# Bias reads at the end of step 4 over two queues, later residual requests, and earlier weight sums in two pairs

## The chip, the cores and the metric

The kernel runs on one core of a Trainium2 chip. The core has TensorE (PE, matrix products; PEld is its weight load), VectorE (DVE), ScalarE (ACT), GpSimd (POOL) and SyncE (SP), each with its own instruction queue that is worked off in order. SP only issues transfers here; ACT issues some too. The metric is the device time of one execution in microseconds; less is better. The profile comes from one further execution, with its own time beside the span that it records.

## The reference

Two layers, each: group normalization of the input (32 groups of channels over the image), attention with relative positions over 32 x 32 = 1024 tokens, output projection, and the input added back. There are 4 images, 768 channels, 12 heads of 64.

```python
def _L0_conv_ref(x, Wqkv, Wproj, bproj, rel_pos_h, rel_pos_w):
    ...
    qkv = x @ Wqkv
    ...
    rel_h = jnp.einsum('bhwc,hkc->bhwk', r_q, Rh)
    rel_w = jnp.einsum('bhwc,wkc->bhwk', r_q, Rw)
    bias = rel_h[..., :, None] + rel_w[..., None, :]
    ...
    scores = scale * jnp.einsum('bqc,bkc->bqk', q, k) + bias
    attn = jax.nn.softmax(scores, axis=-1)
    out = jnp.einsum('bqk,bkc->bqc', attn, v)
    ...
    return out @ Wproj + bproj
...
x = x + _L0_conv_ref(_gn(x), L0_conv_Wqkv, L0_conv_Wproj, L0_conv_bproj, L0_conv_rel_pos_h, L0_conv_rel_pos_w)
x = x + _L1_conv_ref(_gn(x), L1_conv_qkv_w, L1_conv_qkv_b, L1_conv_proj_w, L1_conv_proj_b, L1_conv_rel_pos_h, L1_conv_rel_pos_w)
```

Layer 1 differs by a bias on q, k and v and by a second factor of the scale. Everything is float32.

## The kernel before

**Pairs and steps.** The work is 8 images in a row (4 of layer 0, then 4 of layer 1), 6 pairs of heads in each: 48 pairs, numbered g = 0 to 47; `pair` is g % 6. A pair has 8 steps n = 0 to 7, one for each 128 query tokens. The main loop (from L719) goes over the 384 units (g, n). It is software pipelined by hand: the order in which the program issues work is the order on every engine, except where dependencies between engines make them wait.

**A step.** In step n of pair g the loop issues, in this order:
- what the lists `early` and `later` hold: a closure put into `later` runs at the start of the step after next, one put into `early` at the start of the next;
- until the change, the requests for weights and residuals of the output projection (`fetch_weights`, L578, and `fetch`, L595);
- `biases` (L454) of the unit two ahead: POOL adds the two relative position terms into a 128 x 1024 score tile;
- `scores` (L468) of the unit one ahead: PE multiplies q and k into PSUM (`ps_s`, two tiles, one for each head), DVE adds the bias and finds the minimum (L484), ACT takes the exponential (L488);
- `read_back` calls kept in `behind` and `behind2`;
- `turn` (L506): DVE transposes the finished weights of unit n into `tb`; in odd steps SP writes `tb` to DRAM (`td`, L521). Between the two heads DVE inverts the next unit's sums (L495);
- `divide` (L497) of the unit one ahead, one head on POOL (L502), one on ACT (L504);
- projections of the next pair and output groups of the image before or of this image, taken from the list `todo` by `take`, as many matmul slices as `shares[n]` says;
- one or two entries of `last`, the copies of the first bias term into place by `rows_axis` on ACT (L431).

**Quarters.** Two steps make a quarter. The quarter is written to DRAM in an odd step and read back turned round (`td` to `pt`, L531) in the second step after for quarters 0 and 2, in the next one for quarters 1 and 3. `weigh` (L536) multiplies quarters 0 and 1 with v at the end of step 6, quarters 2 and 3 at the end of step 2 of the next pair. So quarter 1 is written in step 3, read back in step 4 and used in step 6.

**Relative positions.** `positions` (L396) of the next pair runs in steps 2 and 3: PE multiplies q with the tables, ACT copies the result out (L418) and writes the part for one axis to DRAM (`tdr`, L420). `diagonals` (L437) then reads that back along diagonals into `rel_of[g][2]`, eight transfers of 32 KB in runs of 128 bytes (L447). Their first reader is `biases` of the next pair's unit 0, on POOL in step 6.

**Output groups.** An image's output projection is cut into groups of 128 channels by 512 tokens; four of them are taken in step 7 of every pair from g = 3 on. Each needs a 256 KB residual (`res`), added on DVE (L638, L640). Tiles of `res` share a pool of four with the copied positions.

**Weights.** For pairs that are not `plain` the projections use combined weights: `sum_weights` (L321) gives an ACT copy (L330) and three POOL sums (L333 to L335). A DVE copy (L274) and the projections of the next pair read them. The first three pairs of image 0 have no output groups.

## Time and profile before

| what | value |
|---|---|
| median of 3 runs | 3508.94 us (3507.96 to 3512.74) |
| the profiled execution | 3509.05 us, span 3507.3 us |
| busy in the span | PE 97%, DVE 75%, POOL 71%, ACT 57% |
| DMA traffic | 1051.56 MB, 300 GB/s on average |
| transfers td, written | 384 on SP, 1024 KB each, 5.9 us from issue to landing |
| transfers pt, read back | 382 on SP, 1024 KB each, 7.7 us |
| transfers rel, bias reads | 380 on SP and 4 on ACT, 32 KB each, 3.1 and 2.2 us |
| transfers tdr | 94 on ACT, 256 KB each, 4.8 us |

In the views, a line of a group gives the kernel's line, engine, operation, what it writes and reads, and how often; then busy time, mean duration, the idle time of the engine just before, and what ended it. In a timeline the first column is the start from the beginning of the span in us, the second the duration of the merged group, and a bracket at the end holds the idle time before it and what ended that. SPq and ACTq are the sequencers that issue transfers; the duration of an issue is not that of the transfer.

### The profile page before, as it was taken

How to read it: one execution, taken by the hardware profiler on the slowest of the kernel's cores; microseconds unless marked ns; L12 is line 12 of the kernel's file. 1: busy time of each engine (PE TensorE's matmuls, PEld its weight loads, DVE VectorE, ACT ScalarE, POOL GpSimd, SP SyncE). 2: the span in 40 equal slices, each digit the busy share in tenths (PEclk: the TensorE clock that was granted, in tenths of full speed). 3: DMA queues.
4: the chain of work that ended last, by engine and by line, in shares of the span. 5: the costliest groups of instructions: out<-in, count | busy, mean ns of one | idle time of the engine just before them, and what ended most of it. 6: DMA issues, size and time to landing. Idle time of an engine off the chain costs nothing.

```text
span 3507.3 us, 56203 instructions
## 1 busy us (share of the span) xinstructions
PE 3404.6 (97%) x20652; PEld 1906.9 (54%) x20652; DVE 2640.3 (75%) x4011; ACT 1992.0 (57%) x3958; POOL 2489.6 (71%) x1510
## 2 busy tenths in 40 slices
PE   6899999999999999999999999999999999999999
PEld 4455555555555555555555555555555555555554
DVE  4687868778688786787777877777876778777776
ACT  3565556555565556556665566555665566555652
POOL 3876687766866769767686766876678766786663
PEclk9999999999999999999999999999999999999999
DMA  3678988898889887888888898888988889888888
GB/s 115 252 274 321 330 288 307 310 323 327 290 302 328 318 317 270 318 320 320 296 288 316 303 324 289 299 312 302 319 305 300 297 304 327 298 303 299 305 292 289
DMA packets 531221, 1051.56 MB, mean 300 GB/s; under 512 B 143872, under 2 KB 206848, under 8 KB 481792
## 3 DMA queue, kind: packets, MB, share of 16 engines
q1 hardware_dynamic: 476448, 1020.53, 81.0%
q10 hardware_dynamic: 54496, 27.43, 2.6%
q8 instruction: 163, 2.67, 0.3%
q14 instruction: 114, 0.93, 0.1%
HBM read 572.73 MB, written 475.10 MB: 299 GB/s over the span
## 4 chain that ended last, share of the span: by engine, by line
PE 66%; ACT 12%; DMA 8%; DVE 6%; POOL 3%; issue 3%; SPq 1%; ACTq 0%; DVEq 0%; POOLq 0%
PE pj L268 17%; PE av L550 14%; PE s L475 13%; PE o L629 13%; PE pv L376 7%; ACT sc L488 6%; DMA pt<-td 5%; ACT rel L431 3%; ACT sc L504 2%; PE tp L408 2%; DMA td<-tb 2%; DVE x L228 1%; DVE sc L484 1%; DVE tb L518 1%; POOL x L346 1%
## 5 line engine op out<-in xcount | busy, mean ns | idle before, releaser
L461 POOL TENSOR_TENSOR sc<-rel,rel 128x1024 f32<-128x1024 f32 x768 | 1553.3, 2086 | 110.3 <-DVE tb L518 67.6
L488 ACT ACTIVATE sc<-sc,sm 128x1024 f32<-128x1024 f32 x768 | 879.7, 1147 | 927.2 <-DVE sm L484 925.5
L518 DVE STREAM_TRANSPOSE tb<-sc 128x1024 f32<-128x1024 f32 x768 | 944.8, 1234 | 145.4 <-DMA td<-tb 143.8
L484 DVE CUSTOM_DVE_ANT_0 sc<-s,sc 128x1024 f32<-128x1024 f32 x768 | 908.3, 1221 | 149.8 <-PE s L475 141.4
L502 POOL TENSOR_SCALAR sc<-sc,sm 128x1024 f32<-128x1024 f32 x384 | 429.5, 1119 | 804.1 <-DVE sm L495 792.0
L268 PE MATMUL pj<-x,w 64*128 64x512 f32 x4140 | 937.3, 596 | 57.1 <-DVE x L228 26.1
L475 PE MATMUL s<-k,q 64*128 64x512 f32 x3072 | 749.0, 597 | 6.1 <-DVE sm L484 5.9
L550 PE MATMUL av<-pt,v 128*64 128x256 f32 x6144 | 707.5, 383 | 22.8 <-DMA pt<-td 22.8
L268 PEld LDWEIGHTS pj<-x,w 64*128 64x128 f32 x4140 | 421.7, 189 | 545.0 <-issue 451.5
L550 PEld LDWEIGHTS av<-pt,v 128*64 128x64 f32 x6144 | 445.4, 138 | 314.1 <-DMA pt<-td 46.5
L504 ACT ACTIVATE sc<-sc,sm 128x1024 f32<-128x1024 f32 x384 | 441.0, 1148 | 173.6 <-DVE sm L495 173.6
L376 PE MATMUL pv<-wv,x 64*128 64x256 f32 x4608 | 515.1, 376 | 6.8 <-DVE k L243 6.8
L376 PEld LDWEIGHTS pv<-wv,x 64*128 64x128 f32 x4608 | 449.5, 187 | 98.1 <-issue 38.0
L629 PE MATMUL o<-attn,wo 128*128 128x512 f32 x1080 | 478.9, 598 | 4.3 <-DMA wo<-in_wo 1.3
L475 PEld LDWEIGHTS s<-k,q 64*128 64x128 f32 x3072 | 291.5, 187 | 295.9 <-issue 261.8
L431 ACT COPY rel<-t 32x64 f32<-32x64 f32 x1504 | 363.4, 242 | 16.5
L629 PEld LDWEIGHTS o<-attn,wo 128*128 128x128 f32 x1080 | 200.3, 190 | 279.7 <-issue 250.4
L418 ACT COPY t<-tp 128x512 f32<-128x512 f32 x188 | 110.1, 585 | 223.1 <-PE tp L408 169.5
L346 POOL TENSOR_TENSOR x<-x,x 64x512 f32<-64x512 f32 x144 | 183.3, 1292 | 39.6 <-ACT x L348 28.7
L495 DVE RECIPROCAL sm<-sm 128x2 f32<-128x2 f32 x384 | 60.1, 156 | 176.4 <-ACT sc L488 172.4
L243 DVE TENSOR_TENSOR k<-pj,k 128x512 f32<-128x512 f32 x173 | 116.3, 681 | 68.8 <-PE pj L268 44.0
L488 ACT ACTIVATION_READ_ACCUMULATOR sc<-sc,sm 128x1 f32 x768 | 143.2, 186 | 0.0
(54 smaller groups left out, 1575.8 us busy)
## 6 DMA issues: line engine op xcount, KB each, us to landing
td<-tb SPq DMA_DIRECT2D x384, 1024.0 KB, 5.9
pt<-td SPq DMA_DIRECT2D x382, 1024.0 KB, 7.7
w<-in_wqk SPq DMA_DIRECT2D x96, 384.0 KB, 4.8
tdr<-t ACTq DMA_DIRECT2D x94, 256.0 KB, 4.8
x<-in_x SPq DMA_DIRECT2D x84, 256.0 KB, 7.4
part<-res SPq DMA_DIRECT2D x84, 256.0 KB, 5.6
res<-part SPq DMA_DIRECT2D x84, 256.0 KB, 7.8
wv<-in_wv SPq DMA_DIRECT2D x24, 768.0 KB, 13.5
```

Of the source, the lines that this page charges most:

```text
L268: nc.tensor.matmul(t[:, a, :], lhsT=w[a][rows, c, :], rhs=x[c][rows, :], start=(c == 0), stop=(c == len(x) - 1),)
L376: nc.tensor.matmul(t[:, a, k, :], lhsT=xs[i // 2 * NC + c][rows, at * P : (at + 1) * P], rhs=w[rows, c, :], start=(c == 0), stop=(c == NC ...
L431: nc.scalar.copy(rel[of, :, j, :], t[of, j, :, at : at + HW])
L461: nc.gpsimd.tensor_tensor(sc.rearrange("p (a k) (u l) -> p a l (k u)", a=4, l=8), rel0[:, h, :].unsqueeze(1).unsqueeze(2).to_broadcast(shape),
L475: nc.tensor.matmul(ps[h][:, cols], lhsT=q[rows, n * P : (n + 1) * P], rhs=k[rows, cols], start=True, stop=True,)
L484: nc.vector.tensor_tensor_reduce(out=sc, in0=ps[h], in1=sc, scale=-scale, scalar=BIG, op0=ALU.add, op1=ALU.min, accum_out=st[:, 0, h : h + 1],
L488: nc.scalar.activation(sc, sc, AF.Exp, bias=st[:, 0, h : h + 1], scale=-1.0, accum_out=st[:, 1, h : h + 1],)
L502: nc.gpsimd.tensor_scalar(sc, sc, st[:, 2, h : h + 1], 1.0, ALU.mult, ALU.mult)
L504: nc.scalar.activation(sc, sc, AF.Copy, scale=st[:, 2, h : h + 1])
L518: nc.vector.transpose(tb[:, :, j, :], sc_of[g, n, h])
L550: nc.tensor.matmul(av[rows, at * 2 * P : (at + 1) * 2 * P], lhsT=v_of[g][:, k, rows], rhs=pt_of[g, quarter, h][:, :, k, :], start=(k == 0) ...
L629: nc.tensor.matmul(t, lhsT=wo_of[im, o, c], rhs=attn_of[im * NP + c, i], start=(c == c0), stop=(c == c1 - 1),)
```

## The change

Three edits. First, `diagonals` of the next pair is put into a list of its own, `diagonal`, which is run at the end of step 4 and no longer at its start; the four reads of the second head are issued by ACT for every pair, not for pair 0 alone. Second, the requests for output weights and residuals stand behind the bias adds, the scores and the read back in their step, and the second pair of residuals is requested in step 6 and no longer in step 5. Third, the weights of the pair two ahead are combined in steps 5 and 6, no longer in 6 and 7, where g is below 3 and the next pair is not plain, which is for pairs 1 and 2.

```diff
--- before.py
+++ after.py
@@ -432,7 +432,7 @@
 
         last.extend([lambda: rows_axis((0, 1)), lambda: rows_axis((2, 3))])
         if i == 1:
-            later.append(lambda: diagonals(g))
+            diagonal.append(lambda: diagonals(g))
 
     def diagonals(g):
         td = t_of[g]
@@ -444,7 +444,7 @@
                     td.tensor, td.offset + HW * y * P + h * D + HW - 1,
                     [[P - 1, HW], [P * P, NT], [1, HW]],
                 )
-                (nc.scalar if h and not g else nc.sync).dma_start(
+                (nc.scalar if h else nc.sync).dma_start(
                     out=rel_of[g][2][32 * y : 32 * y + 32, h, :, :], in_=src
                 )
 
@@ -655,7 +655,7 @@
 
 
 
-    early, mid, later, last, behind, behind2 = [], [], [], [], [], []
+    early, mid, later, last, diagonal, behind, behind2 = [], [], [], [], [], [], []
 
     def run(todo):
         while todo:
@@ -705,7 +705,7 @@
         take(todo, NC)
         mid.pop(0)()
         run(last)
-        later.pop()()
+        run(diagonal)
         take(todo, 2 * NC)
         run(early)
         run(later)
@@ -746,11 +746,6 @@
             run(early)
             early, later = later, early
 
-            upto = 4 * (pair % 3) + 3
-            if n in (2, 4, 5) and (im, pair) >= (0, 3):
-                upto -= 2 if n == 4 else 0
-                (fetch_weights if n == 2 else fetch)(place[((im, 0) if pair >= 3 else (im - 1, 1)) + divmod(upto, 2)])
-
             ask = [divmod(g + 3, NP)] if n == 1 else []
             if im == 0 and pair < 3:
                 ask = [(0, 2 * pair + n // 4)] if n in (1, 4) else []
@@ -766,6 +761,11 @@
                 scores(*units[at + 1])
             run(behind)
             behind, behind2 = behind2, behind
+
+            upto = 4 * (pair % 3) + 3
+            if n in (2, 4, 6) and (im, pair) >= (0, 3):
+                upto -= 2 if n == 4 else 0
+                (fetch_weights if n == 2 else fetch)(place[((im, 0) if pair >= 3 else (im - 1, 1)) + divmod(upto, 2)])
             if pair == 3 and n in stages and not end:
                 stages[n]()
             share = shares[n]
@@ -782,11 +782,15 @@
                         take(todo, 3)
                         share -= 3
                     apply(c % NC, c // NC)
-            if g + 2 < NPAIR and not plain(g + 2) and n in (6, 7):
-                if n == 6:
+            if g + 2 < NPAIR and not plain(g + 2):
+                k = n - (5 if g < 3 and not plain(g + 1) else 6)
+                if k == 0:
                     combine = sum_weights(g + 2)
-                combine[n - 6]()
+                if k in (0, 1):
+                    combine[k]()
             take(todo, share)
+            if n == 4:
+                run(diagonal)
             for k in range(min(len(last), 2 if n == 3 else 1)):
                 last.pop(0)()
             if pair == NP - 2 and n == 7 and not end:
```

## The prediction

> **What bounds the kernel now.** I read the page's busy times first, then the waits, then timelines of steps 4 to 7 of two pairs. From the page, busy times and the row of the weighted sums:

> ```profile
> PE 3404.6 (97%) x20652; PEld 1906.9 (54%) x20652; DVE 2640.3 (75%) x4011; ACT 1992.0 (57%) x3958; POOL 2489.6 (71%) x1510
> ...
> L550 PE MATMUL av<-pt,v 128*64 128x256 f32 x6144 | 707.5, 383 | 22.8 <-DMA pt<-td 22.8
> ```

> TensorE is idle for 102.7 us of 3507.3; only that, and matmuls slowed by idling, can be won. I measured each step on TensorE from one score block's start to the next. In a common pair of either layer the steps take 6.97, 10.33, 9.87, 6.87, 6.90, 6.90, 8.87, 12.41 us, again and again; above all step 6, where quarters 0 and 1 are weighed, varies. Over pairs 1 to 46 its excess above 8.87 sums to 44.7 us: 26.1 in the eight pairs numbered 4, 18.6 in the rest (0.5 each). Step 7 adds 6.1 in four of the pairs 4. Pair 28 shows why; timeline of SP, then of TensorE (start, duration, last the wait):

> ```profile
> 2099.96 1.79 SPq L521 DMA_DIRECT2D td<-tb  x2
> 2101.84 3.42 SPq L117 DMA_DIRECT2D x<-mid  x3
> 2105.35 4.95 SPq L447 DMA_DIRECT2D rel<-tdr  x8
> 2111.10 0.35 SPq L131 DMA_DIRECT2D w<-in_wqk  x1
> 2111.55 0.85 SPq L608 DMA_DIRECT2D res<-mid  x2
> 2112.46 0.97 SPq L531 DMA_DIRECT2D pt<-td  x2
> ```

> ```profile
> 2117.45 4.22 PE L550 MATMUL av<-pt,v 128*64 128x256 f32 x34
> 2123.72 5.35 PE L550 MATMUL av<-pt,v 128*64 128x256 f32 x30 [2.05 <-DMA pt<-td]
> ```

> Quarter 1's transposed weights went out at 2099.96 and 2101.42 and had landed at 2107.45, but SP asked for them back at 2112.46, after eight bias reads and two residuals; the second landed at 2123.68 and TensorE waited. After the wait 30 matmuls took 5.35 us; the granted clock of that step is 0.87.

> [...] bias reads cost 0.45 us each on SP (median) and 0.47 on ACT (the first pair's four). [...] ACT at pair 4's first position block:

> ```profile
> 368.47 0.59 ACT L418 COPY t<-tp 128x512 f32<-128x512 f32 x1 [3.24 <-PE tp L408]
> 371.54 0.37 ACTq L420 DMA_DIRECT2D tdr<-t  x1
> 371.95 0.58 ACT L418 COPY t<-tp 128x512 f32<-128x512 f32 x1 [2.89 <-DMA td<-tb]
> ```

> The copy ended at 369.05, yet the issue came at 371.54, when an unrelated write (td, landed 371.46) was done. By the transfers' records all 1,992 transfers of SP and ACT share eight semaphores in rotation: each issue waits until the transfer eight before it has landed. SP shows it too: three of the bias reads above are issued at the landings of the three x loads eight places earlier.

> **The change, part by part.** Time 0 is the start of step 4's scores in pair 26 (1961.25).

> (a) Bias reads. Before: eight issues, 6.24 us of SP, then the read back at 8.4 and 8.8, landed 17.0 and 19.6; quarter 1 is first used at about 19.2 (13.8 for step 6, 1.9 for scores, 3.5 for quarter 0). After: the writes land at 3.6 and 6.1, and the reads go then. A read with little ahead lands 5.7 to 6.4 us after issue (2089.39 to 2095.77), the second follows 2.7 later: 9.6 and 12.3. That is 7 us early: step 6's wait goes, 44.7 us, with step 7's 6.1.

> The price is on ACT. Four issues of 0.47 are 1.9 us a pair, 47 x 1.9 = 88 in all, behind step 4's division and ahead of eight bias copies and step 5's exponentials. ACT in pair 26:

> ```profile
> 1968.04 1.15 ACT L504 ACTIVATE sc<-sc,sm 128x1024 f32<-128x1024 f32 x1 [0.23 <-DVE sm L495]
> 1969.10 2.01 ACT L431 COPY rel<-t 32x64 f32<-32x64 f32 x8
> 1971.88 1.15 ACT L488 ACTIVATE sc<-sc,sm 128x1024 f32<-128x1024 f32 x1 [0.78 <-DVE sm L484]
> ...
> 1978.34 1.15 ACT L488 ACTIVATE sc<-sc,sm 128x1024 f32<-128x1024 f32 x1 [2.69 <-DVE sm L484]
> ```

> The 0.78 and 2.69 us of idle hide 1.9. They don't hide the semaphores. Ahead of the eight bias reads now stand, in order of issue: tdr, td, td, w, pt, pt, res, res. So the first four reads find their semaphores free, and the last four wait for pt, pt, res, res: 9.6, 12.3 and, residuals landing 0.65 apart, 12.9, 13.6. SP is ready for its four at about 7 (just after the second read and two residual issues), ACT at 7.9 to 9.4; so the last place is probably ACT's. Its fourth issue ends near 14.1 instead of the block being over at 9.8. Then copies 2.0 (16.1), two exponentials 2.4 (18.5; before 13.0). Behind them: VectorE's reciprocal and second transpose 1.35, four value adds 1.65 (21.5), the two score evacuations 2.4 (h = 0 done 22.7, h = 1 23.9; before 15.8 to 18.2). TensorE wants the second score bank at 22.9: 1.0 us late. The lateness still stands on VectorE in step 7, where the third or fourth output group waits 0.3 to 0.9 for its bank. I take 1.4 a pair. A precedent bounds it below: in pairs numbered 3 the exponentials of step 5 already end at 15.7 (a square root in step 4), and TensorE's step 6 is at its 8.87 there in pairs 21 and 39. So the first 3 to 4 us of delay are free.

> In pairs numbered 4 VectorE also normalizes inputs in steps 6 and 7 and is the tighter engine: evacuation in step 7 ended 6.5 us before the next scores in pair 28 (33.1, 39.6). With the hold near 15 it ends at about 34.2, so 40.7 against a best of 35.1: 5.6 lost. Pairs numbered 5 have a step 4 of 13.2 us: no loss.

> POOL needs the reads for step 6's bias adds at 14.4; they land near 16. Its four units of work there fill 7.78 of 9.48 us and the sums are used only at 25: nothing, unless the reads are over 6 us late.

> (b) Operands. Two residual requests move from step 5 to step 6, and all behind the read back. Eight issues in a pair stay eight. Before, SP stood up to 3.5 us at L608 for bias copies on ACT (40.8 us in all), hidden because the next write waits for VectorE anyway. Residuals requested near 15 to 21 land by 29; the adds that use them come after 30. Cost 0; if that cover went, 0.7 a group.

> (c) Weights. Pairs 1 and 2 alone: one ACT copy (0.83) and three POOL sums (1.80 each) come a step sooner. Their step 7 is 3.4 us, with no output groups. POOL, VectorE and TensorE at pair 2:

> ```profile
> 213.51 1.79 POOL L335 TENSOR_TENSOR w<-w,w 64x768 f32<-64x768 f32 x1
> 215.27 3.95 POOL L461 TENSOR_TENSOR sc<-rel,rel 128x1024 f32<-128x1024 f32 x2
> ```

> ```profile
> 215.34 4.09 DVE L274 COPY w<-w 64x384 f32<-64x384 f32 x1 [3.38 <-POOL w L335]
> ```

> ```profile
> 219.48 9.84 PE L268 MATMUL pj<-x,w 64*128 64x512 f32 x36 [3.51 <-DVE w L274]
> ```

> The sums would end at 207, the copy could start when VectorE is free at 212.4, and would again run beside bias adds[...] (4.09 us, median 0.59). So it ends by 216.5 instead of 219.4: 3 us a pair, 6 in all. Bounds: 0 and 14 (step 1 is 17.56 there, 10.33 elsewhere).

> **Sum, against the profiled run's 3509.05** (span 3507.3 and 1.75 around it; the median of three is 3508.94, the same). Off: 44.7 + 6.1 + 6. On: 31 pairs at 1.4 = 43, seven at 5.6 = 39, the last loaded pair (46) 1.4: 84. Net +27: 3536 us.

> **Rivals.**
> - *ACT goes first.* If ACT's four stand before SP's, or its last no later than the place that waits for the second pt (12.3), the exponentials end by 17.1 and nearly all is covered. SP then waits instead, with nothing urgent behind it. 3509.05 - 56.8 + 3 = 3455. The rotation of semaphores is fixed before the run, and in the old trace it departs from the order of issue times by up to 3 us between the two engines; ACT would need some 1.5. This is the case on the other side of no change.
> - *The two cancel.* A hold that ends near 13, or only in some kinds of pair: half of the 84 and all of the gain would be 3494, three quarters 3515; I put it at 3504.
> - *VectorE can't catch up.* If lateness outlives step 7 into the next pair, or the idle lowers the clock as in pair 28 (0.87), 3 a pair rather than 1.4 gives about 3586.
> - *The read back is no earlier.* Were it limited by its bytes, nothing would be won; but 12.3 against 19.6 leaves 7 us.

> **How the numbers follow.** ACT held 0.57 (own range 3512 to 3568, from 0.6 to 2.4 us a pair), ACT first 0.25, cancelling 0.12, no catching up 0.06. Some 0.2% (7 us) is what a measurement can tell from no change: of the held case 0.06 lies within it, of the cancelling one 0.06 within and 0.03 on each side. Faster 0.28, same 0.12, slower 0.60. For 8 in 10 the range must reach into the fast case: 3452 to 3566.

> **What would show it.** Right: the reads of pt in step 4 issued within 1 us of the writes' landing; step 6's wait on pt near 0; gaps of 3 to 5 us on ACT ahead of L447; waits of scores on VectorE growing from 6 us to over 25. Wrong: no gap on ACT at L447, a hold under 3 us, or waits of POOL on the bias reads.

## The result and the profile after

The changed kernel takes 3654.59 us (median; 3653.83 to 3655.51), the kernel before, run beside it, 3510.84. The ratio is 1.0409, with a 95% interval of 1.0391 to 1.0427: 144 us slower, where 27 were predicted, and outside the range of 3452 to 3566.

From the page of the changed kernel, the busy times and the rows that answer to those of before:

```profile
PE 3472.9 (95%) x20652; PEld 1913.6 (52%) x20652; DVE 2648.2 (73%) x4011; ACT 1997.1 (55%) x3958; POOL 2486.2 (68%) x1510
...
L475 PE MATMUL s<-k,q 64*128 64x512 f32 x3072 | 792.2, 610 | 46.5 <-DVE sm L484 46.1
L550 PE MATMUL av<-pt,v 128*64 128x256 f32 x6144 | 707.8, 388 | 48.1 <-DVE v L391 47.0
...
L431 ACT COPY rel<-t 32x64 f32<-32x64 f32 x1504 | 363.7, 242 | 262.1 <-DMA rel<-tdr 207.6
```

Three things are to be seen. The weighted sums hardly wait for the read-back (1.2 us, once; 22.8 us before): that part worked. They wait 47.0 us for value tiles from VectorE instead, and the scores wait 46.1 us for score banks (5.9 before). And TensorE is *busy* 68.3 us longer with the same 20,652 matmuls: its mean granted clock fell from 0.996 to 0.979. The bias copies on ACT stand behind 262.1 us of idle time, against 16.5 before. The rows of the scores and of the copies before the change:

```profile
L475 PE MATMUL s<-k,q 64*128 64x512 f32 x3072 | 749.0, 597 | 6.1 <-DVE sm L484 5.9
L431 ACT COPY rel<-t 32x64 f32<-32x64 f32 x1504 | 363.4, 242 | 16.5
```

Measured step by step on TensorE, as in the prediction, the two traces differ by 144.5 us: 66.6 in step 6, 67.5 in step 7, 8.4 in step 1, little elsewhere. An odd pair shows the chain. Pair 25, timeline of SP and then of ACT (start, duration, engine, line, last the wait); its step 4 starts at 1965.80:

```profile
1968.70 3.66 SPq L531 DMA_DIRECT2D pt<-td  x2
1972.46 0.95 SPq L608 DMA_DIRECT2D res<-part  x2
1973.46 2.08 SPq L447 DMA_DIRECT2D rel<-tdr  x4
```

```profile
1974.48 0.37 ACT L388 COPY v<-pv 128x256 f32<-128x256 f32 x1 [0.49 <-DVE v L391]
1975.85 6.59 ACTq L447 DMA_DIRECT2D rel<-tdr  x4
1982.49 2.02 ACT L431 COPY rel<-t 32x64 f32<-32x64 f32 x8 [7.63 <-DMA rel<-tdr]
```

SP's four reads go out in 2.08 us. ACT's four, of the same size, take from 1975.85 to 1982.44. By the transfers' records they are issued at 1975.85, 1980.34, 1981.49 and 1982.14; the transfers eight places before them, two read-backs and two residuals, land at 1975.83, 1980.32, 1981.47 and 1982.12. ACT is held until 16.6 us into step 4, with eight copies and two exponentials behind it. TensorE in the same pair, and then in pair 26:

```profile
1981.40 7.13 PE L550 MATMUL av<-pt,v 128*64 128x256 f32 x64
1991.06 4.91 PE L475 MATMUL s<-k,q 64*128 64x512 f32 x8 [2.53 <-DVE sm L484]
1995.90 12.13 PE L629 MATMUL o<-attn,wo 128*128 128x512 f32 x24
```

```profile
2057.71 2.81 PE L550 MATMUL av<-pt,v 128*64 128x256 f32 x24
2063.09 6.22 PE L550 MATMUL av<-pt,v 128*64 128x256 f32 x40 [2.57 <-DVE v L391]
```

In the odd pair TensorE idles 2.53 us for the score bank; then eight score matmuls take 4.91 us (1.99 in pair 26) and 24 output matmuls 12.13 (10.57). Those two excesses, 2.92 and 1.56, are all of the 4.49 us by which step 7 is over its 12.41; 1.14 of it is the second score bank, which VectorE frees at 1992.14, one evacuation after the first (an evacuation is VectorE's reading of a finished bank, which frees it: the first ends at 1990.99, and the scores start at 1991.06). In the even pair TensorE stops in the middle of the weighted sums, for a value tile. The granted clock in four of these stretches (window; length; busy time of each engine; then the clock, the DMA share and GB/s):

```profile
2063.09:2069.24 6.15, 6.15 (x40) 3.59 (x41) 5.45 (x9) 4.00 (x6) 4.79 (x4) 0.72 1.02 343
1979.59:1988.53 8.94, 8.94 (x74) 5.09 (x70) 1.31 (x2) 5.71 (x14) 1.32 (x2) 1.00 0.47 149
1991.06:1995.90 4.84, 4.82 (x9) 1.46 (x9) 4.69 (x8) 4.34 (x6) 3.39 (x3) 0.62 0.99 324
1995.90:2007.96 12.06, 12.06 (x26) 5.12 (x25) 8.41 (x14) 3.53 (x5) 7.66 (x6) 0.87 0.66 260
```

In pair 25 the clock is 1.00 ahead of the idle time and 0.62 and 0.87 behind it; in pair 26 it is 0.72 behind it. In pair 28, shown of before, all 64 weighted sums are now one run; and for part (c), pair 2's projection waits 1.43 us for the combined weight instead of 3.51 (TensorE again, two stretches):

```profile
229.39 2.85 PE L268 MATMUL pj<-x,w 64*128 64x512 f32 x12 [1.43 <-DVE w L274]
...
2208.68 7.13 PE L550 MATMUL av<-pt,v 128*64 128x256 f32 x64
```

### The profile page after: what moved, and what is told of

Its sections match the earlier page's. It is cut to its first block, busy times and chain, and to the rows that moved or that the text cites. A ratio compares the mean times of both kernels' runs of the same rounds, so it can differ in the third digit from the quotient of the medians.

```text
span 3652.2 us, 56214 instructions
## 1 busy us (share of the span) xinstructions
PE 3472.9 (95%) x20652; PEld 1913.6 (52%) x20652; DVE 2648.2 (73%) x4011; ACT 1997.1 (55%) x3958; POOL 2486.2 (68%) x1510
## 4 chain that ended last, share of the span: by engine, by line
PE 27%; DMA 8%; ACT 8%; DVE 4%; issue 2%; POOL 2%; SPq 0%; ACTq 0%; DVEq 0%; POOLq 0%
PE o L629 7%; PE pj L268 6%; PE av L550 6%; PE s L475 6%; ACT sc L488 4%; DMA td<-tb 3%; DMA pt<-td 2%; ACT rel L431 2%; DVE tb L518 1%; PE tp L408 1%; ACT sc L504 1%; DMA rel<-tdr 1%; DMA res<-part 1%; DVE x L228 1%; DVE sc L484 1%
## 5 line engine op out<-in xcount | busy, mean ns | idle before, releaser
L461 POOL TENSOR_TENSOR sc<-rel,rel 128x1024 f32<-128x1024 f32 x768 | 1548.0, 2085 | 72.7 <-DMA rel<-tdr 65.8
L488 ACT ACTIVATE sc<-sc,sm 128x1024 f32<-128x1024 f32 x768 | 879.5, 1146 | 783.2 <-DVE sm L484 780.9
L484 DVE CUSTOM_DVE_ANT_0 sc<-s,sc 128x1024 f32<-128x1024 f32 x768 | 908.4, 1220 | 157.9 <-PE s L475 146.0
L268 PE MATMUL pj<-x,w 64*128 64x512 f32 x4140 | 940.5, 595 | 64.2 <-DVE x L228 26.5
L475 PE MATMUL s<-k,q 64*128 64x512 f32 x3072 | 792.2, 610 | 46.5 <-DVE sm L484 46.1
L550 PE MATMUL av<-pt,v 128*64 128x256 f32 x6144 | 707.8, 388 | 48.1 <-DVE v L391 47.0
L268 PEld LDWEIGHTS pj<-x,w 64*128 64x128 f32 x4140 | 412.5, 189 | 565.8 <-issue 467.1
L550 PEld LDWEIGHTS av<-pt,v 128*64 128x64 f32 x6144 | 440.0, 140 | 345.2 <-issue 65.5
L504 ACT ACTIVATE sc<-sc,sm 128x1024 f32<-128x1024 f32 x384 | 441.0, 1148 | 199.9 <-DVE sm L495 199.9
L629 PE MATMUL o<-attn,wo 128*128 128x512 f32 x1080 | 499.9, 618 | 8.0 <-DVE attn L559 3.9
L431 ACT COPY rel<-t 32x64 f32<-32x64 f32 x1504 | 363.7, 242 | 262.1 <-DMA rel<-tdr 207.6
L475 PEld LDWEIGHTS s<-k,q 64*128 64x128 f32 x3072 | 306.3, 190 | 355.8 <-issue 258.8
L629 PEld LDWEIGHTS o<-attn,wo 128*128 128x128 f32 x1080 | 207.5, 197 | 305.7 <-issue 251.7
L495 DVE RECIPROCAL sm<-sm 128x2 f32<-128x2 f32 x384 | 59.9, 156 | 412.2 <-ACT sc L488 407.6
L418 ACT COPY t<-tp 128x512 f32<-128x512 f32 x188 | 110.1, 586 | 226.9 <-PE tp L408 177.0
L346 POOL TENSOR_TENSOR x<-x,x 64x512 f32<-64x512 f32 x144 | 184.0, 1298 | 39.6 <-ACT x L348 28.7
L488 ACT ACTIVATION_READ_ACCUMULATOR sc<-sc,sm 128x1 f32 x768 | 143.3, 187 | 0.0
```

The lines of the kernel that those rows point to most:

```text
L268: nc.tensor.matmul(t[:, a, :], lhsT=w[a][rows, c, :], rhs=x[c][rows, :], start=(c == 0), stop=(c == len(x) - 1),)
L431: nc.scalar.copy(rel[of, :, j, :], t[of, j, :, at : at + HW])
L461: nc.gpsimd.tensor_tensor(sc.rearrange("p (a k) (u l) -> p a l (k u)", a=4, l=8), rel0[:, h, :].unsqueeze(1).unsqueeze(2).to_broadcast(shape),
L475: nc.tensor.matmul(ps[h][:, cols], lhsT=q[rows, n * P : (n + 1) * P], rhs=k[rows, cols], start=True, stop=True,)
L484: nc.vector.tensor_tensor_reduce(out=sc, in0=ps[h], in1=sc, scale=-scale, scalar=BIG, op0=ALU.add, op1=ALU.min, accum_out=st[:, 0, h : h + 1],
L488: nc.scalar.activation(sc, sc, AF.Exp, bias=st[:, 0, h : h + 1], scale=-1.0, accum_out=st[:, 1, h : h + 1],)
```

## The experiments

The theory: ACT is held at its reads because each waits for the transfer eight places before it, and what stands behind it on ACT reaches VectorE and TensorE late ("the hold"). In the traces of the kernel before and of the changed one, each of eight semaphores serves 249 transfers, and in either trace none of the 1,984 issues that follow another transfer on their semaphore starts before that one has landed; the closest starts 0.016 us after it. The main rivals: the four issues cost ACT their own 1.9 us a pair; the later place of the reads costs; (b) or (c) costs.

### Is it ACT's queue, and is it the hold?

**All eight reads on SP**, nothing else undone (all_sp):

```diff
-(nc.scalar if h else nc.sync).dma_start(
+(nc.scalar if h and not g else nc.sync).dma_start(
```

> The changed kernel, but all eight bias reads of a pair stand on SP's queue, still at the end of step 4. Theory (the hold): ACT's four issues wait for the landings of both read-backs and both residuals, and everything behind them on ACT, VectorE and TensorE is late; off ACT the hold is gone, step 6's wait on the read-back stays gone, and the kernel should take 3455 to 3470 us, with the granted clock back at 0.99 or above. Rival (the later place): what costs is that the reads are at the end of step 4, so that POOL's bias adds come late; then about 3650, as in the changed kernel. Rivals (moved fetches, earlier sums): their loss would stay too, and the time would be above 3500.

3475.84 us, a ratio of 0.9898 (0.9884 to 0.9913) to the kernel before, clock 0.996. The reads stand at the same late place and land as late (medians of 17.5 to 17.9 us into step 4 in pairs numbered 0 to 3; 17.7 to 18.1 after the change), and step 6 takes 8.87 to 8.90 us in every pair but those numbered 5. So neither the late place nor (b) nor (c) is the loss: the second queue is. It is also 1% better than the kernel before. It missed the expected 3455 to 3470 by 6 us; why is told below.

**One read of the eight on ACT**, the last (one_on_act):

```diff
-(nc.scalar if h else nc.sync).dma_start(
+(nc.scalar if h and (y == 3 or not g) else nc.sync).dma_start(
```

> The changed kernel, but only the last of the eight bias reads stands on ACT, seven on SP. Theory (the hold): it is the last place in the rotation that decides, and one issue that waits for the last residual holds ACT almost as long as four do: 3600 to 3655 us. Rival (the price of the issues themselves, 0.47 us each on ACT): one issue instead of four leaves about a quarter of the loss, 3490 to 3510 us.

3579.06 us (1.0183; 1.0166 to 1.0200): between the two, so neither number was right. The trace says why. In pairs numbered 0, 2 and 4 ACT's one read has a place whose predecessor has long landed; in pairs 1 and 3 it has the last place. Timeline of ACT in pair 26, then in pair 25, of this kernel:

```profile
2016.10 0.41 ACTq L447 DMA_DIRECT2D rel<-tdr  x1
2017.08 2.01 ACT L431 COPY rel<-t 32x64 f32<-32x64 f32 x8
```

```profile
1949.39 0.33 ACTq L447 DMA_DIRECT2D rel<-tdr  x1
1949.76 2.02 ACT L431 COPY rel<-t 32x64 f32<-32x64 f32 x8 [7.76 <-DMA rel<-tdr]
```

The same single issue costs nothing in the one and 7.76 us of ACT in the other. Pairs 1 and 3 lose as much as with four reads on ACT, the even ones nothing in steps 6 and 7. It is the wait, not the work of issuing.

**The first head's reads at the old place**, so that other transfers stand eight places before ACT's four (first_head_early):

```diff
-diagonal.append(lambda: diagonals(g))
+if g:
+    later.append(lambda: diagonals(g, (0,)))
+diagonal.append(lambda: diagonals(g, (1,) if g else (0, 1)))
...
```

> The changed kernel, but SP's four bias reads (first head) stand at the old place at the start of step 4 and ACT's four (second head) alone at its end. The work of ACT is the same four issues in the same place; what changes is what stands eight places before them: the first reads, not the read-backs and residuals. Theory (the hold): ACT waits at most for the weights' and old transfers' landings, the time falls to 3455 to 3500 us. Rivals (price of the issues on ACT, the late place): still about 3640 to 3660 us.

3480.63 us (0.9912; 0.9897 to 0.9926), as the theory has it: four issues on ACT, in the same place of its program, and the loss is gone. The idle time ahead of ACT's copies (L431) is 106.0 us in all, not 262.1.

**Part (b) undone** (no_fetch_move): the requests stand ahead of the scores again, with this condition:

```diff
...
-if n in (2, 4, 6) and (im, pair) >= (0, 3):
+if n in (2, 4, 5) and (im, pair) >= (0, 3):
...
```

> The changed kernel without part (b): residuals requested at the old place, ahead of the read-back; the bias reads still on two queues at the end of step 4. Theory: the hold doesn't come from (b); the read-back, behind two residuals, lands later and ACT's places wait for it longer, so the loss is the same or larger: 3650 to 3690 us. Rival (the hold comes from the moved residuals): the loss shrinks by half or more, to under 3590.

3635.72 us (1.0355; 1.0339 to 1.0370): a loss a little smaller than expected, and far from half. It gives the cleanest comparison, since one kernel has both cases. ACT in pair 25, then in pair 26:

```profile
1968.01 8.10 ACTq L447 DMA_DIRECT2D rel<-tdr  x4
...
2040.66 2.36 ACTq L447 DMA_DIRECT2D rel<-tdr  x4
```

The four issues take 8.10 us, and pairs 1 lose 5.7 us each; they take 2.36, and pairs 2 lose nothing. All of it in one table: the end of ACT's last issue, in us after step 4's scores begin (median), and the loss of a pair against the kernel with the same (b) and all reads on SP (mean over the pairs of a number from pair 6 on, all steps; seven pairs of each, six of number 5, without the last pair of the program):

| pair number | 0 | 1 | 2 | 3 | 4 | 5 |
|---|---|---|---|---|---|---|
| changed: end of ACT's issues | 14.4 | 16.4 | 14.7 | 16.1 | 9.1 | 20.1 |
| loss a pair | 5.6 | 5.4 | 5.0 | 6.7 | -0.2 | 0.3 |
| (b) undone: end | 8.9 | 17.0 | 9.5 | 16.9 | 9.3 | 19.7 |
| loss a pair | 2.0 | 5.7 | 0.0 | 8.2 | 1.8 | 0.4 |
| one read on ACT: end | 7.2 | 16.5 | 7.2 | 16.0 | 6.6 | 19.4 |
| loss a pair | 1.6 | 5.5 | 0.1 | 6.9 | -0.5 | -0.2 |

A hold to 9.5 costs little, one to 14 or more costs 5 to 8 us (in pairs 4 pair 46 is the odd one out: with (b) undone it alone loses 6.0, the others 1.0 on average). The long step 4 of pairs 5 hides theirs, except that pairs 0, behind them, pay 1.6 to 1.9 us on average in step 1 (pair 6 pays 3.8 after the change), where TensorE waits for combined weights from POOL: 8 waits of 11.2 us in all after the change, one of 2.8 with the reads on SP. Which place a read of ACT has stands in its instruction (in pair 25 of the changed kernel the trace gives its four the semaphores 103, 105, 106 and 107, those of the two read-backs and the two residuals). In odd pairs ACT still copies value tiles in step 4 (L388 above) and all four of its reads come behind SP's; in pair 26 three of the four came ahead. That the one causes the other was not tried.

### How the hold becomes 5 to 7 us of TensorE

**Value tiles ahead of the transposes** on VectorE in step 5 (values_first):

```diff
...
+if n == 5:
+    first = 6
 first = min(first, share)
...
```

> The changed kernel, but in step 5 VectorE evacuates the value tiles ahead of the reciprocal and transposes that wait for ACT. ACT's hold is untouched. Theory: in pairs with even numbers a part of the hold reaches TensorE through the value tiles that step 6's weighted sums read; step 6 of these pairs falls from about 13.3 to about 10 us, and step 7's wait on the scores stays or grows: 3570 to 3630 us. Rival (step 6 is late because of the transposes or the clock, not the values): no change beyond 10 us.

3644.01 us (1.0378; 1.0362 to 1.0393), above the expected 3570 to 3630. Step 6 of even pairs fell further than expected, from 12.6 and 13.8 us to 8.9 in pairs 0 and 2, 60 us in all; pair 26 of this kernel:

```profile
2052.10 7.13 PE L550 MATMUL av<-pt,v 128*64 128x256 f32 x64
```

In the changed kernel VectorE stood in pair 26 until ACT's exponentials came, and evacuated the value tiles behind them:

```profile
2060.95 0.17 DVE L495 RECIPROCAL sm<-sm 128x2 f32<-128x2 f32 x1 [5.96 <-ACT sc L488]
2061.04 1.23 DVE L518 STREAM_TRANSPOSE tb<-sc 128x1024 f32<-128x1024 f32 x1
2062.18 0.39 DVE L390 TENSOR_TENSOR v<-pv,v 128x256 f32<-128x256 f32 x1
2062.61 0.42 DVE L391 TENSOR_TENSOR v<-pv,v 128x256 f32<-128x256 f32 x1
```

So the wait inside the weighted sums is the value tiles', held up behind a reciprocal and a transpose that need ACT's exponentials. But most came back: 24.5 us in step 1 of pairs 0, 13.8 in step 7. Other order on VectorE moves the lateness; it doesn't take it away.

**The idle time filled.** Two kernels add matmuls whose result nothing reads, in pairs 1 and 3, between step 6's sums and the next scores. With 22 of them (fill_idle), and with 10 (fill_less: `range(5 ...)`):

```diff
...
+for k in range(11 if n == 2 and first == 0 and half == 0 and g > 5 and g % 6 in (1, 3) else 0):
+    for h in range(2):
+        rows = slice(h * D, (h + 1) * D)
+        nc.tensor.matmul(
+            bank[rows, 4 * P : 6 * P], lhsT=v_of[g][:, k % NT, rows],
+            rhs=pt_of[g, 1, h][:, :, k % NT, :], start=True, stop=True,
+        )
```

> The changed kernel with work added that nothing reads: in pairs numbered 1 and 3, from pair 7 on, 22 more matmuls of the weighted sums' shape (about 0.11 us each, 2.4 in all), into an unused half of the same bank, between step 6's sums and the next scores, where TensorE stands idle for about 2.5 us. Theory (lower clock after the idle): step 7 of these pairs takes 16.9 instead of 12.41 us because the idle time is followed by matmuls at a lower granted clock; with the idle filled, step 7 goes back to 12.4 to 13.6 while step 6 stays at 10.5 to 12: about 40 us less, 3605 to 3625 us, with a granted clock above 0.985. Rival (the slow matmuls come from something else that is late, or from the traffic): step 7 stays at 16.9, and the time is that of the changed kernel or up to 30 us more.

> The changed kernel with 10 added matmuls in place of 22 in the idle time of step 6 in pairs numbered 1 and 3 (22 took 4.75 us, so 0.216 each, 2.2 us in all); nothing reads them. Theory [...]: step 6 of these pairs stays near its 10.9 to 11.8 us, since the scores wait for VectorE as before, and step 7 goes from 16 to about 12.4, at most 13.6: 40 to 50 us below the changed kernel, 3605 to 3615 us. Rival (22 matmuls helped because they delayed the scores past something else that is late): step 7 stays near 16 us, time within 15 us of the changed kernel's.

With 22: 3632.38 us (1.0351; 1.0336 to 1.0367), clock 0.988. A matmul of the program is two in the profile, so each took 0.216 us, twice the expected figure, and step 6 grew to 13.6 us; yet step 7 fell from 16 to 12.4 or 12.6 in all fourteen pairs, and the kernel is some 20 us faster than the changed one with more work. With 10: 3622.19 us (1.0319; 1.0304 to 1.0334). Both times are 7 us above what was expected, and steps 6 and 7 went as expected, but for the longer step 6 with 22. Pair 25 with 10:

```profile
1969.49 2.33 PE L558 MATMUL av<-pt,v 128*64 128x256 f32 x20
1972.28 3.13 PE L475 MATMUL s<-k,q 64*128 64x512 f32 x8 [0.46 <-DVE sm L484]
1975.33 10.85 PE L637 MATMUL o<-attn,wo 128*128 128x512 f32 x24
```

The first row is the added work. The scores come as late as before: step 6 of these pairs is 11.2 and 11.8 us on average, against 10.7 and 11.8. But the 24 output matmuls take 10.85 instead of 12.13, and step 7 is over its 12.41 by 12.7 us in all, instead of 51.4. So the slow stretch came from TensorE's standing idle, and not from the lateness itself: 38.7 us in these fourteen pairs. What is left is mostly about 1.14 us a pair, in the score block (3.13 instead of 1.99): the wait for the second score bank.

### The parts alone

**(c) alone** (sums_only) is the last part of the diff put into the kernel before:

```diff
-if g + 2 < NPAIR and not plain(g + 2) and n in (6, 7):
+if g + 2 < NPAIR and not plain(g + 2):
+    k = n - (5 if g < 3 and not plain(g + 1) else 6)
```

> The kernel before, with part (c) alone: weights of the first pairs combined a step sooner. Prediction: 6 us less, so a ratio of 0.998 (bounds 0 and 14 us); pairs 2 and 3 each some 3 us shorter in step 1. Rival [...]: no gain or up to 10 us more.

3505.51 us, 0.9989 (0.9980 to 0.9997): 4 us, with 1 to 7 in the interval. Pairs 2 and 3 are 2.2 and 3.0 us shorter. As predicted.

**(b) alone** (fetch_only), in the kernel before; the requests stand behind the read-back:

```diff
...
-if n in (2, 4, 5) and (im, pair) >= (0, 3):
+if n in (2, 4, 6) and (im, pair) >= (0, 3):
...
```

> The kernel before, with part (b) alone: the operand requests behind the read-back, those of step 5 in step 6. Prediction: nothing, within 5 us. Rival (it is what delays the read-back or the output groups): 20 us or more slower.

3482.90 us, 0.9923 (0.9908 to 0.9938): 27 us faster, where nothing was expected. SP in pair 26:

```profile
1953.54 0.98 SPq L531 DMA_DIRECT2D pt<-td  x2
1954.62 0.94 SPq L608 DMA_DIRECT2D res<-part  x2
```

Before, two residuals were requested just ahead of the read-back, which then landed 17.0 and 19.6 us into step 4; now it goes first and lands at 14.2 and 17.8, and step 6's sum over 8.87 falls by 35.8 us. (b) removes the very stall that (a) was to remove.

**(a) undone** (no_reads_move: reads at the start of step 4 on SP, with (b) and (c)), and **(a) on SP without (b)** (all_sp_no_fetch):

```diff
-diagonal.append(lambda: diagonals(g))   # no_reads_move alone
+later.append(lambda: diagonals(g))
-(nc.scalar if h else nc.sync).dma_start(   # both
+(nc.scalar if h and not g else nc.sync).dma_start(
... (all_sp_no_fetch has the requests at their old place as well)
```

> The changed kernel without part (a): all eight bias reads on SP at the start of step 4, as before; (b) and (c) stay. Theory: (b) alone took about 27 us off, because two residual transfers no longer stand ahead of the read-back, and (c) 4 us; the sum is about 3478 us, and (a) has nothing left to win: step 6 is already near 8.9 us. Rival (the moved reads are needed too): 3490 us or more.

> The kernel before with part (c) and with the reads at the end of step 4, all on SP, but residuals requested at the old place. It tells what the later place of the reads is worth alone. Theory: the read-back goes at the landing of its writes but behind two residuals, so most of step 6's wait goes: 3475 to 3485 us, nearly what (a) on SP and (b) give together. Rival (only (b) brings the read-back forward): 3500 to 3510 us.

3474.33 us (0.9897; 0.9881 to 0.9914), and 3483.45 (0.9925; 0.9910 to 0.9940). So the later place of the reads, on one queue and with (c), is worth about 26 us, (b) about as much, and both no more than (b) with (c). The stall can be won once. No version tried is better than no_reads_move and all_sp, which can't be told apart.

**Two queues at the old place** (two_queues_old_place), in the kernel before:

```diff
-(nc.scalar if h and not g else nc.sync).dma_start(
+(nc.scalar if h else nc.sync).dma_start(
```

> The kernel before, with the second head's four bias reads on ACT, all eight still at the start of step 4. SP's block of reads is halved (3.1 instead of 6.2 us), so the read-back is issued at the landing of its writes; ACT pays the same four issues, but where the transfers eight places before have landed. Theory (the hold, not the second queue, costs): 3455 to 3480 us. Rival (four issues on ACT cost TensorE time wherever they stand, 1.9 us a pair): 3500 us or more.

3545.41 us (1.0102; 1.0086 to 1.0119): my expectation failed. SP's block got no shorter, because two of its reads now had the places of the two writes and were issued at their landings (4.57 and 7.03 in pair 26); the read-back went out at 9.05 and 9.53, later than the 8.35 and 8.83 of before. And 23.3 us were lost in step 5 of pairs 5 from pair 11 on. ACT in pair 29, and TensorE behind it:

```profile
2207.68 1.01 ACT L431 COPY rel<-t 32x64 f32<-32x64 f32 x4
2208.60 1.40 ACTq L447 DMA_DIRECT2D rel<-tdr  x3
2210.04 1.15 ACT L488 ACTIVATE sc<-sc,sm 128x1024 f32<-128x1024 f32 x1 [1.35 <-DMA rel<-tdr]
```

```profile
2215.15 7.14 PE L376 MATMUL pv<-wv,x 64*128 64x256 f32 x48 [2.27 <-DVE k L243]
```

The three issues follow each other without a gap, once SP's own reads eight places before have landed (10.77 to 11.40 us into step 4); ACT idles 1.35 us, which is no more than three issues take. TensorE then waits 2.27 us (0.95 before), and the same 48 matmuls take 7.14 us instead of the 5.35 of step 4: 3.0 us lost. In other pairs 5 a hold comes on top, and ACT idles up to 2.93 us. So the rival is right in part: in pairs 5 the issues alone cost some 3 us. In pairs 0 to 3 it fails: ACT's issues delay step 5's score evacuation by 1.2 us, and these pairs lose between -0.6 and 0.2 us each. Adding a queue changed which transfers wait for which, on both queues.

## Why the prediction was wrong

- **That ACT is held by the places of read-backs and residuals**: right. The close times in pair 26 are partly luck: the last issue came at 14.05 us (predicted: its end near 14.1), the exponentials end at 18.7 (18.5), the score evacuation at 24.0 (23.9). But ACT's last place was behind the second read-back, which landed at 14.03 and not at 12.3, and not behind the second residual, from which the 14.1 was worked out. ACT in that pair:

```profile
2048.97 7.49 ACTq L447 DMA_DIRECT2D rel<-tdr  x4
2056.50 2.02 ACT L431 COPY rel<-t 32x64 f32<-32x64 f32 x8 [6.47 <-DMA pt<-td]
```

- **That step 6's stall goes, 44.7 us**: right. With the hold taken away (all_sp) step 6 is 44.6 us shorter. **That step 7's 6.1 go**: wrong; there it is 17.2 longer. In pairs 4 TensorE's wait moves to the output groups, which wait for VectorE's evacuations (15.0 us at L629 in all_sp, 2.8 before); in pair 28 these stand behind three input normalizations. Of 19.3 us won in step 6 of pairs 4 from pair 10 on, 12.3 return in step 7. And the end of the program, behind the last scores, is 3.1 us longer, for a reason that stays open. So the gain was 32.5 us in the trace, not 56.8.
- **"I take 1.4 a pair"**: the step that failed. The hold cost 177 us (the changed trace against all_sp), not 84, and 5.0 to 6.7 a pair in pairs 0 to 3 (4.5 in pair 26 itself). It was mis-sized because three terms were missed. First, pair 26 isn't typical: in odd pairs all four of ACT's reads have the late places, and the hold ends some 1.7 us later. Second, in even pairs TensorE needs value tiles in the middle of step 6, and VectorE evacuates them behind the late exponentials; the working listed those "four value adds" and did not ask who reads them. Third, TensorE ran slower after standing idle (in pair 25 a granted clock of 0.62 and 0.87 behind 2.53 us of it), which cost some 3.4 us there, and 38.7 us in the fourteen pairs that fill_less filled: the prediction had seen that in pair 28 and named it in a rival, with a chance of 0.06 and no price of its own.
- **"Pairs numbered 4: 5.6 lost"**: wrong. All four of ACT's reads there have predecessors landed by 8.6 us (pair 28), and the hold ends at 9.1 (except pair 46): the rival *ACT goes first* is what happens in these pairs. **Pairs 5, no loss**: right (0.3 a pair), but for pairs 0 after them.
- **POOL and the late reads, nothing**: right in pairs 0 to 3. In all_sp the reads are as late, and POOL does wait for them, 82.5 us beside the long wait at the start (1.3 before); steps 6 and 7 of these pairs still take 8.87 and 12.41 or 12.42. What they do to pairs 4 is not shown.
- **(b), cost 0**: wrong by 27 us, to the good when alone. The working priced SP's time and the residuals' own readers, and not the transfers that stand behind them. With ACT's reads in place it is to the bad: undoing (b) is 19 us faster, since the even pairs' reads then get places that are free.
- **(c), 6 us**: right; 4 measured.
- **The signs named beforehand**: in pair 26 the read-backs go out 0.07 and 0.06 us after the landings of their writes, and the scores' waits are 46.1 us; both came. The gap on ACT is 6.5 us in pair 26 and 7.6 in pair 25, and not 3 to 5.

## What to carry to other kernels

Before a transfer is put on a second queue, list the transfers that stand before it in the semaphores' rotation (eight places in these traces) and when each lands, in every kind of iteration, and ask what stands behind the issue on that engine. Where a delay reaches an engine, follow every tile that the delayed engine produces to its first reader. A stall of TensorE can cost more than its length (in pair 25 of the changed kernel, 3.4 us behind an idle time of 2.5); and two edits that remove the same stall add up to one.

## What the runs showed of the hardware

In the traces of the kernel before and of the changed one, every stretch of a lower granted clock is granted half (0.5; 9 and 30 of them). Output matmuls start 0.85 us apart in the slow stretch of pair 25 and 0.43 behind it. After the change, from pair 7 on, idle times of 1.41 to 3.66 us ahead of step 7 were followed by slow output matmuls in ten of eleven odd pairs (in the eleventh the slow stretch ended with the scores), and 0.78 to 0.96 in none of three. It isn't a sharp limit: in the weighted sums of pairs 6, 12 and 18 of the same kernel, idle times of 2.44, 3.47 and 2.69 us had no slow stretch behind them. Pair 12, TensorE:

```profile
1018.27 2.81 PE L550 MATMUL av<-pt,v 128*64 128x256 f32 x24
1024.56 4.54 PE L550 MATMUL av<-pt,v 128*64 128x256 f32 x40 [3.47 <-DVE v L391]
```

The 40 sums take 4.54 us here, 6.22 in pair 26.
